# The softmax denominators of a first attention layer: reciprocal on VectorE, or exponential of the negative logarithm on ScalarE

## Chip, cores and metric

The kernel runs on one core of a Trainium2 chip. The metric is the device time of one execution in microseconds (us), shown as the median of several runs.

## What is computed

The reference chains eight blocks, an attention and a feed-forward block in each of four layers, over 8 sequences of 512 tokens with 128 features. Every block is preceded by a layer normalisation and added to its input. Only the first is touched, an attention with 16 heads of 8 features:

```python
scores = einsum('bhqd,bhkd->bhqk', wq, wk) * scale
scores = where(mask, neg, scores)
attn = softmax(scores, axis=-1)
outs.append(einsum('bhqk,bhkd->bhqd', attn, wv))
```

Queries go in windows of 128. The mask is the upper triangle counted from the first key, so query i of any window reaches keys 0 to i of the sequence, never more than its first 128 keys. The other blocks that matter here are a mixture of 8 small experts (two chosen per token), a linear attention with 64 features, whose output is divided by a normaliser, and a mixture of 16 experts (one per token) with a shared expert.

## The kernel before

The first stage (function l0_l1_ffn) takes the eight sequences b through the first four blocks in a software pipeline. Its loop counts steps t; eight steps belong to one sequence, two for each r = 0 to 3; one r covers four heads, one in each quarter of 32 partitions. Generators do the parts, and each step advances the live ones by one yield: `scores` (early), `exps` and `add_up` in the loop itself, `give` (tails), `experts` (gates), `features` (linear), `router` (routers), and `shared` as filler (experts1). The framework turns the program into one queue per engine, with semaphores between them; the order within a queue need not be the written one.

Steps of one sequence, with their lines:

- `scores`: normalise, project, then for each 128 queries PE makes scores (L489), ACT copies them out of PSUM (L495, sm), POOL masks them (L496), DVE takes the maxima (L500). The maxima are transposed (L507, mxT).
- `exps(b, r)`: PE makes the transposed scores less their maximum (L519, sT), ACT takes the exponential (L526, eT, two of 128x1024), POOL masks (L528).
- `add_up(b, r, i)`: PE multiplies eT by the values (i = 0, vq) or by ones (i = 1, own) into two PSUM banks, o0 and o1 (L542). After r = 3, o0 is the weighted sum of the values and o1 holds the softmax sums, repeated over each head's eight rows.
- `give(b)`: DVE inverts o1 into rd (L550) and multiplies by o0 into aT (L552); PE projects (L557), DVE adds to the residual (L558) and takes statistics.
- `experts(b)`: among its steps a Sqrt on ACT (L604), the choice of two experts on DVE (L566 to L577, ending in w, L635), the exponential of w (L637), DVE steps that write the gate tile we (L645), a Silu (L658).
- `features(b)`: the linear attention; its normaliser is clamped (L767) and inverted by DVE (L770), then POOL multiplies (L771).
- `router(b)`: small DVE steps count the rows (L814 to L819), then POOL scatters them with four indirect DMAs (L823).

The scores, the exponentials and the features all go through one PSUM tag of two pairs of banks ("two"). Ten DMAs of zeros (L842) and the loads of later weights (L848) stand on SP's queue in the same stage; the first ten read tile we.

ScalarE holds one table of functions at a time. Where the next function needs another one, the profile has a row ACT_TABLE_LOAD, with the line of the instruction that it serves.

Of the kernel before, what the change touches and what calls it, by code (L numbers as in the profile page):

```python
# [17 lines left out]
AF = mybir.ActivationFunctionType  # L18
# [48 lines left out]
def eight_layers(ctx: ExitStack, tc: tile.TileContext, w: dict, out: bass.AP):  # L67
    nc = tc.nc
# [171 lines left out]
    def cols(c):  # L240
        return slice(c * P, (c + 1) * P)

    def stats(b, mv, x=None):

        x = X[b] if x is None else x
        for c in range(C):
            st = small.tile([P, 6], F32, tag="bn", name="bn", bufs=4)
            nc.vector.bn_stats(st, x[:, c, :])  # L248
            nc.vector.bn_aggr(mv[:, b * C + c, :], st)
# [20 lines left out]
    def l0_l1_ffn():  # L270
# [28 lines left out]
        with ExitStack() as es:  # L299
# [27 lines left out]
            def mm_four():  # L327
                return mm_tile().rearrange("p (c d) -> p c d", c=C)
# [69 lines left out]
            with ExitStack() as es1:  # L398
# [112 lines left out]
                sums_of = {}  # L511
# [35 lines left out]
                def give(b):  # L547
                    ready.pop(b)
                    rd = work.tile([P, S], F32, tag="rd", name="rd", bufs=2)
                    nc.vector.reciprocal(rd, sums_of.pop((b, 1)))  # L550
                    aT = work.tile([P, S], F32, tag="aT", name="aT", bufs=2)
                    nc.vector.tensor_tensor(aT, rd, sums_of.pop((b, 0)), ALU.mult)  # L552
                    yield True
                    yield True
                    pr = mm_four()
                    for k in range(C):
                        nc.tensor.matmul(pr[:, k, :], aT[:, cols(k)], a0["Wo"], start=True, stop=True)  # L557
                    nc.vector.tensor_tensor(X[b], X[b], pr, ALU.add)  # L558
                    stats(b, mv1)
                    gates.append(experts(b))  # L560
                    yield True
# [274 lines left out]
                while t < N * NB or waiting or early or tails or gates or linear or routers:  # L836
# [12 lines left out]
                    b, s = divmod(t, N)  # L849
                    r = s // 2  # L850
                    if s % 2 == 0:
                        if 0 <= b < NB:
                            waiting[b, r] = exps(b, r)
                        step(tails)
                        step(gates)
                        old = (b, r - 1) if r else (b - 1, 3)
                        if old in waiting:
                            add_up(*old, 0, waiting.pop(old))
                            if old[1] == 3:
                                tails.append(give(old[0]))  # L860
                                step(tails)
                        step(routers)
                        step(linear)
                        step(early)
                    else:
                        step(early)
                        step(tails)
                        step(gates)
                        step(routers)
                        step(linear)  # L870
                        if (b, r) in waiting:
                            add_up(b, r, 1, waiting[b, r])
# [1047 lines left out]
```

## Time and profile before

| | |
|---|---|
| median of 3 runs | 1764.63 us (1763.21 to 1764.7) |
| the profiled execution, its own time | 1759.35 us |
| its span, first to last instruction | 1757.6 us |
| busy, share of the span | PE 86%, DVE 67%, ACT 45%, POOL 39% |
| mean granted TensorE clock | 0.94 |

Busy time is an average over stages with different limits; the first stage ends, with the last scatter of `router`, near 660 us, and its attentions near 480 us. A row of the timeline has the start, the length, the engine, the line, the operation with its tiles, and in brackets the engine's idle time just before it with what ended that. Rows of the groups give the total busy time, the mean of one instruction in ns, and the idle time before them.

### The profile page before, as it was taken

The page shows a single profiled execution, that of the slowest core. Times are in us where ns is not written, and L with a number is a line of the kernel's source. Part 1 is how long each engine was busy: PE and PEld are TensorE (multiplying, and loading weights), DVE is VectorE, ACT ScalarE, POOL GpSimd, SP SyncE. Part 2 cuts the span into 40 slices and gives each one's busy share as a digit, 9 for nine tenths or more (in the row PEclk, how much of TensorE's full clock was granted, in tenths as well). Part 3 has the DMA queues.
Part 4 walks back from the last instruction along what each step waited for, and adds up shares of the span by engine and source line. Part 5 has one row for each costly group of instructions (what it writes and reads, how often), then busy time and mean ns, then how long its engine had stood idle before and what let it go on. Part 6 is the DMA issues. An engine that isn't in the chain of part 4 may idle for free.

```text
span 1757.6 us, 23028 instructions
## 1 busy us (share of the span) xinstructions
PE 1505.0 (86%) x8389; PEld 675.3 (38%) x8389; DVE 1169.2 (67%) x2274; ACT 787.2 (45%) x1144; POOL 677.2 (39%) x729
## 2 busy tenths in 40 slices
PE   6978898899898786767999899787988988998877
PEld 2322334344444433544555454332222222333335
DVE  5657546545564443235677675569999999998865
ACT  4545645456454341224233123025655655655644
POOL 5644343344332122021112523425556546632670
PEclk8989998989989998987899899899999999999999
DMA  7991000000000002731554374354444444443301
GB/s 256 384 340 28 1 1 1 13 19 12 6 13 19 18 31 84 219 89 27 131 123 116 98 157 104 91 120 130 132 132 130 129 131 130 129 121 100 81 13 31
DMA packets 98946, 170.96 MB, mean 97 GB/s; under 512 B 11592, under 2 KB 41680, under 8 KB 94736
## 3 DMA queue, kind: packets, MB, share of 16 engines
q1 hardware_dynamic: 94112, 158.20, 32.0%
q0 software_dynamic: 3568, 9.18, 1.7%
q10 hardware_dynamic: 1152, 2.10, 0.4%
q8 instruction: 66, 1.08, 0.2%
q14 instruction: 48, 0.39, 0.1%
HBM read 116.50 MB, written 52.95 MB: 96 GB/s over the span
## 4 chain that ended last, share of the span: by engine, by line
PE 48%; DVE 24%; issue 9%; ACT 6%; SPq 6%; POOL 5%; DMA 2%; DVEq 0%; POOLq 0%; ACTq 0%
DVE h L1827 11%; PE key L1581 5%; PE acc L1559 5%; SPq L842 5%; PE bx L1816 3%; PE sT L519 2%; PE gu L366 2%; PE mm L262 2%; PE Z L1627 2%; PE mm L1187 2%; PE o L542 1%; DVE zx L1635 1%; PE mm L673 1%; PE qq L731 1%; DVE rd L770 1%
## 5 line engine op out<-in xcount | busy, mean ns | idle before, releaser
L1827 DVE TENSOR_TENSOR_SCAN h<-a,bx 128x1024 f32<-128x1024 f32 x192 | 426.3, 2267 | 18.1 <-PE bx L1816 18.1
L1822 ACT ACTIVATE a<-dr,nA 128x1022 f32<-128x1022 f32 x192 | 219.4, 1146 | 213.4 <-DVE h L1827 213.3
L1816 PE MATMUL bx<-gx,wb 64*128 64x512 f32 x768 | 217.9, 658 | 65.9 <-DVE h L1827 63.0
L1272 POOL TENSOR_TENSOR gx<-gx,xk 128x1024 f32<-128x1024 f32 x32 | 75.4, 2357 | 211.7 <-DMA gx<-du_d 208.4
L1581 PE MATMUL key<-xT,L_ffn_keys 128*128 128x512 f32 x256 | 137.4, 619 | 21.9 <-DVE act L1585 21.9
L1816 PEld LDWEIGHTS bx<-gx,wb 64*128 64x128 f32 x768 | 63.6, 191 | 199.4 <-DVE h L1827 157.1
L1559 PE MATMUL acc<-act,L_ffn_values 128*128 128x512 f32 x256 | 133.2, 604 | 0.0
L1585 DVE SCALAR_TENSOR_TENSOR act<-key,gate 128x512 f32<-128x512 f32 x128 | 86.4, 685 | 48.1 <-PE key L1581 38.4
L500 DVE TENSOR_REDUCE mx<-sm 128x8 f32<-128x1024 f32 x64 | 75.9, 1212 | 56.1 <-POOL sm L496 56.1
L1627 PE MATMUL Z<-h,wc 64*32 64x512 f32 x1536 | 110.8, 630 | 1.1 <-DVE h L1827 1.1
L528 POOL TENSOR_SCALAR_AFFINE_SELECT eT<-eT 128x1024 f32<-128x1024 f32 x64 | 68.6, 1095 | 102.3 <-ACT eT L526 102.2
L1370 POOL DMA_INDIRECT back<-f_out,back_at x32 | 30.8, 963 | 168.4 <-DVE bn L248 138.1
L496 POOL TENSOR_SCALAR_AFFINE_SELECT sm<-sm 128x1024 f32<-128x1024 f32 x64 | 69.0, 1095 | 67.4 <-ACT sm L495 67.0
L495 ACT COPY sm<-sc 128x1024 f32<-128x1024 f32 x64 | 62.6, 1014 | 46.5 <-PE sc L489 27.6
L526 ACT ACTIVATE eT<-sT 128x1024 f32<-128x1024 f32 x64 | 62.0, 1019 | 39.8 <-PE sT L519 39.6
L1581 PEld LDWEIGHTS key<-xT,L_ffn_keys 128*128 128x128 f32 x256 | 47.5, 197 | 74.3 <-issue 37.8
L1347 ACT COPY oT<-acc 128x512 f32<-128x512 f32 x8 | 4.7, 586 | 158.0 <-PE acc L1559 158.0
L1559 PEld LDWEIGHTS acc<-act,L_ffn_values 128*128 128x128 f32 x256 | 49.5, 195 | 60.5 <-issue 60.0
L489 PE MATMUL sc<-kb,qT 32*128 32x512 f32 x256 | 55.1, 698 | 18.9 <-ACT eT L526 10.2
L519 PE MATMUL sT<-qT,kb 32*128 32x512 f32 x256 | 55.7, 683 | 9.1 <-ACT sm L495 7.3
L248 DVE BATCH_NORM_STATS2 bn<-x 128x6 f32<-128x128 f32 x224 | 56.2, 272 | 6.3 <-DMA x<-in_L_attn_hidden_states 5.3
L1053 POOL TENSOR_TENSOR rstd<-rstd,minus_half 128x4 f32<-128x4 f32 x27 | 28.0, 1039 | 77.6 <-DVE rstd L1052 77.4
(460 smaller groups left out, 3076.1 us busy)
## 6 DMA issues: line engine op xcount, KB each, us to landing
f_in<-we SPq DMA_DIRECT2D x10, 3584.0 KB
gate<-gates SPq DMA_DIRECT2D x128, 256.0 KB
dr<-dt_d SPq DMA_DIRECT2D x32, 1024.0 KB
gx<-du_d SPq DMA_DIRECT2D x128, 128.0 KB
wt<-in_L_ffn_experts SPq DMA_DIRECT2D x48, 192.0 KB
xk<-xh_d SPq DMA_DIRECT2D x32, 256.0 KB
xg<-f_in SPq DMA_DIRECT2D x48, 64.0 KB
f_out<-ys SPq DMA_DIRECT2D x12, 256.0 KB
```

The source lines that it names most:

```text
L496: nc.gpsimd.affine_select(out=sm, in_=sm, compare_op=ALU.is_ge, fill=-1e30, base=0, pattern=[[0, 8], [-1, P]], channel_multiplier=1,)
L500: nc.vector.tensor_reduce(mx[:, c, 2 * i : 2 * i + 2, 0:4], sm.rearrange("p (q r) k -> p q r k", q=2), AX.X, ALU.max, negate=True,)
L519: nc.tensor.matmul(halves[q // 2][:, q % 2, :], lhs[quad(q), r, :], rhs[quad(q)], start=(k == 0), stop=(k == 1),)
L842: nc.sync.dma_start(rows_in[per * (t - 1) : per * t, :].rearrange("(p n j) d -> p n (j d)", p=P, j=4), we.rearrange("p c k e -> p (c k e)" ...
L1272: nc.gpsimd.tensor_tensor(gx, gx, xk.unsqueeze(1).to_broadcast([P, 2, S]), ALU.mult)
L1559: nc.tensor.matmul(acc, f2_v[:, j, :], act, start=(j == 0), stop=(j == J - 1))
L1581: nc.tensor.matmul(key, f2_k[:, 2 * j : 2 * j + 2, :], xT, start=True, stop=True)
L1585: nc.vector.scalar_tensor_tensor(act, key, 0.0, gate[:, j % 2, :], ALU.max, ALU.mult)
L1627: nc.tensor.matmul(zs[q][32 * j : 32 * j + 32, i, :], wcf[half, g, :], hs[j // 2][half, j % 2, :], start=(g == 0), stop=(g == G - 1),)
L1816: nc.tensor.matmul(bx[:, k, :], wbf[half, g, :], gx[half, j, :], start=True, stop=True,)
L1822: nc.scalar.activation(a[:, :, 1:], dr[:, 2 * j : 2 * j + 2, 1:], AF.Exp, scale=nA[:, q, g : g + 1],)
L1827: nc.vector.tensor_tensor_scan(h.rearrange("p r t -> p (r t)"), a.rearrange("p r t -> p (r t)"), bx.rearrange("p r t -> p (r t)"), 0.0, AL ...
```

## The change

In `give`, DVE's reciprocal of the softmax sums becomes two ACT instructions: the natural logarithm from PSUM into rd, then in place the exponential of its negative, since exp(-ln s) = 1/s. The multiply that follows stays on DVE. The diff has this one place; the second attention's reciprocal (L770) is as before.

```diff
                 def give(b):
                     ready.pop(b)
                     rd = work.tile([P, S], F32, tag="rd", name="rd", bufs=2)
-                    nc.vector.reciprocal(rd, sums_of.pop((b, 1)))
+
+                    nc.scalar.activation(rd, sums_of.pop((b, 1)), AF.Ln)
+                    nc.scalar.activation(rd, rd, AF.Exp, scale=-1.0)
                     aT = work.tile([P, S], F32, tag="aT", name="aT", bufs=2)
                     nc.vector.tensor_tensor(aT, rd, sums_of.pop((b, 0)), ALU.mult)
```

## The prediction

> **What bounds the kernel now.** I read the table of stages first, then the rows of the one line that the change takes away, then the timeline around each of its eight executions, and last the chain of work that ended last. The change touches only the first stage, the one in which the attentions of the first layer run through their eight sequences, from 0 to about 480 us. These are the stage's rows after the first transfers; the columns are length, then busy time of PE, PEld, DVE, ACT and POOL with instruction counts, granted clock, DMA share and GB/s:
>
> ```profile
> 60.00:132.00 72.00, 60.20 (x347) 21.79 (x346) 46.40 (x97) 35.26 (x42) 37.90 (x41) 0.88 1.02 356
> 132.00:165.00 33.00, 26.52 (x136) 9.32 (x137) 22.45 (x41) 18.07 (x24) 13.80 (x14) 0.90 0.14 35
> 165.00:220.00 55.00, 48.53 (x298) 20.92 (x297) 33.09 (x80) 31.80 (x40) 24.19 (x26) 0.94 0.00 1
> 220.00:294.00 74.00, 67.04 (x427) 28.41 (x424) 38.09 (x96) 37.67 (x46) 26.82 (x29) 0.91 0.00 1
> 294.00:369.00 75.00, 67.38 (x439) 29.93 (x440) 41.17 (x115) 38.55 (x50) 31.66 (x34) 0.93 0.04 11
> 369.00:440.00 71.00, 66.63 (x468) 29.26 (x469) 36.85 (x113) 39.98 (x51) 29.32 (x32) 0.98 0.05 16
> ```
>
> Two regimes are seen. Until about 121 us the DMA engines are full (share 1.02). After that PE is busy some 90% of the time, and DVE and ACT a little over half each. So neither the engine that gets lighter nor the one that gets heavier is the bound on average. What counts is where PE stands still because an ACT or DVE result is late, and those places lie at the turn from one sequence to the next, where the reciprocal is. The turn of the sixth sequence, from the timeline of all engines (start, length, engine, line, idle time before it and who ended it):
>
> ```profile
> 340.59 3.35 DVE L550 RECIPROCAL rd<-o 128x512 f32<-128x512 f32 x1
> ...
> 348.87 0.16 DVE L635 TENSOR_TENSOR w<-oh_m 128x4 f32<-128x4 f32 x1
> ...
> 350.23 0.69 PE L710 MATMUL kq<-bf,row 32*128 32x256 f32 x2 [2.35 <-ACT eT L526]
> ```
>
> and from the timeline of ACT alone:
>
> ```profile
> 344.88 1.28 ACT L637 ACT_TABLE_LOAD   x1
> 349.06 0.20 ACT L637 ACTIVATE w<-w 128x4 f32<-128x4 f32 x1 [2.90 <-DVE w L635]
> 349.17 1.92 ACT L526 ACTIVATE eT<-sT 128x1024 f32<-128x1024 f32 x2
> ```
>
> DVE does the 3.35 us reciprocal, then the small steps that choose the experts, and their last, w (L635), comes at 348.87. ACT holds the small exponential of w (L637) ahead of the two large exponentials (L526), so it stands idle for 2.90 us, and PE for 2.35 us behind it. The reciprocal is thus on the path at some turns, though DVE is half idle.
>
> **What goes.** Eight reciprocals, all alike:
>
> ```profile
> L550 DVE RECIPROCAL rd<-o x8: 3345/3348/3358, 64.5 to 467.3; 128x512 f32<-128x512 f32 x8
> ```
>
> DVE loses 8 x 3.35 = 26.8 us. The second attention's reciprocal (L770, also 3.35 us) stays: the diff has one place only.
>
> **What comes.** Eight Ln and eight Exp of 128x512 on ACT. No Ln is in the trace. The nearest rows, with the table loads, are these:
>
> ```profile
> L637 ACT ACT_TABLE_LOAD x7 | 9.0, 1283 | 0.1
> ...
> L1202 ACT ACTIVATE z<-z 128x512 f32<-128x512 f32 x8 | 5.1, 632 | 0.0
> ...
> L265 ACT COPY mxT<-mm 128x512 f32<-128x512 f32 x8 | 4.7, 587 | 8.0 <-PE mm L262 8.0
> ```
>
> Ln reads PSUM and writes SBUF like the copy: 0.59 us. Exp works in place in SBUF like L1202: 0.63 us. Both could lie between the copy's 0.59 and the 0.69 of an activation from PSUM with a bias column (L1201, 688 ns); eight pairs differ by 1.3 us at most by that, which I neglect. The larger part is the table loads, 1.28 us each. Before every change among Sqrt, Exp and Silu the trace has a load, 76 in all. I assume Ln has a table of its own, so one load before Ln and one before the Exp. Seven of the eight places are lucky for the second: L604 (Sqrt) loads before the reciprocal and the next exponential reloads behind it (second to seventh sequence: 91.39 and 98.22, 139.93 and 146.76, 189.08 and 200.38, 255.20 and 269.89, 329.58 and 344.88, 402.46 and 413.86), so for six of them the reload only moves forward. The first place stands among exponentials (+2), and in the eighth the next load is for Silu (475.00), so its reload is extra too (+2). Ten loads more, 86. ACT gets 6 x 2.50 + 2 x 3.78 = 22.6 us.
>
> What a switch costs besides the load: at 139.93 the load starts 0.02 us after the activation before it ends, and the Sqrt starts 0.01 us after the load, so nothing. The Trainium skill (ScalarE: Activation LUTs, What ACT_TABLE_LOAD costs) adds a drain of about 1.38 us to every switch, 2.66 us in all; this trace doesn't show it. By that figure the cost summed below would be some 3.5 us higher (half of 1.38 at five turns) and the time about 1763; as the rows around 139.93 leave no room for it, it gets no chance of its own.
>
> **Sequence by sequence.** The first two turns (64.5 and 93.9 us) lie ahead of this row:
>
> ```profile
> 120.82 0.26 DVE L645 TENSOR_TENSOR we<-oh 128x96 f32<-128x96 f32 x1 [12.62 <-DMA L_ffn_shared_gate_w<-in_L_ffn_shared_gate_w]
> ```
>
> DVE stands 12.6 us until the transfers that read tile we are through. Those run back to back on SP's queue (L842, some 9.4 us each) and wait for no engine's work here. What ACT loses (3.78 and 2.50) or DVE gains (2 x 3.35) before that is swallowed; I cost it at 0. If that cover were gone, it would be between -6.7 and +6.3.
>
> *Gain at the others.* The most that can be had is the idle time of ACT in front of w, and no more than 3.35: third sequence 3.35 (idle 6.37 at 154.41), fourth 1.48 (at 203.15), fifth 2.99 (at 274.16), sixth 2.90, seventh 0 (there the exponentials went at 415.15 ahead of w). In the eighth the reciprocal is itself a link of the chain that ended last:
>
> ```profile
> 467.36 3.26 DVE rd L550
> 470.65 0.59 DVE x L777
> ```
>
> Behind it DVE makes the row numbers (L814 to L819) for POOL's four scatters (L823, 475.31 to 484), and L639, DVE's L645 and PE at 485.94 (idle 6.69) wait behind those: 3.35. Together 14.1. In the fifth and sixth, two reduces (L500) that wait for POOL's masks also stand ahead of w, so what is late next is POOL; I take half there, 1.50 and 1.45. That leaves 3.35 + 1.48 + 1.50 + 1.45 + 3.35 = 11.1 us.
>
> *Cost at the others.* Ln waits for the sums of PE (L542, own), then stands in ACT's queue with the masked scores' copies (L495), the copies L694 and the large exponentials behind it; POOL's masks, DVE's maxima and, through the two PSUM pairs that scores and exponentials share, PE wait for those. ACT's idle gaps around the place are 1.76 + 0.54 in the third sequence before its long wait, 5.1 in the fourth, 3.0, 4.1 and 2.7 in the next three, so 2.50 would nearly fit each time; but single gaps are 0.3 to 1.8 us and a load is 1.28. Bounds: 0 when all fits, 2.50 x 5 = 12.5 when nothing does. I take half, 6.3, being as near to one as to the other. In the eighth a gap of 3.02 us before 471.13 takes most of it: 0 (bound 3.78). The multiply L552 waits for Exp now; Ln, load and Exp in a row take 2.5 us against 3.35, so it is not later as long as ACT starts at once.
>
> **Sum.** -11.1 + 6.3 = -4.8 us. Against the profiled execution (1759.35, of which 1757.6 is the span) 1754.5; the median shown is 5.3 higher, so 1764.6 - 4.8 = **1759.8**. All routers end before the expert stage can start, so a shift of this stage should reach the end whole.
>
> **Rivals.**
> *ACT becomes the late one (slower).* The pieces don't fit the gaps, and POOL's masks, not the reciprocal, hold w. Each turn then pays up to 2.50 and the last 3.78: 16.3 at most, 1780.9, and some 1773 if half is paid and nothing gained. It decides from the point where the copies L495 after a turn start over 1.3 us later while L637 still idles as long. For it: DVE waits for POOL sm and POOL for ACT sm through most of the stage (36.1 and 35.3 us between 160 and 440). Against: ACT's gaps add up to more than 2.50 at four turns of five.
> *It cancels.* Gain and cost within 3 us: 1764.6. For it: PE is 90% busy, so at most some 8 us a sequence can be won at all.
> *One load serves both.* If the load before Ln brings a table that holds Exp too, no load is added in the six middle turns and two in the other places: 78 loads, 1.22 us of ACT a turn, half paid at five turns 3.1, and 11.1 - 3.1 = 8.0 faster, 1756.6. The loads of before can't tell, as they have no Ln. The Trainium skill (ScalarE: Activation LUTs, Table sets: the hidden batching unit) names a set with both and counts one load for ln followed by exp; no run here shows which set is taken.
> *The order changes.* PE's instructions do not run in the written order (at 337.6 to 340.2 the products L542 of the old sequence run ahead of L519 of the new one, written first), so the program's order follows expected durations, and new ones can shuffle a turn. One misplaced w costs 6.4 us, as in the second and third sequence; either sign.
>
> **How the numbers follow.** Forecast 0.40 (0.36 faster, 0.04 same), ACT late 0.32 (slower), cancels 0.16 (same), one load 0.07 (faster), order 0.05 (0.02 faster, 0.03 slower). Faster 0.45, same 0.20, slower 0.35, where same is within 0.2%, 3.5 us, about what can be told from no change here. The forecast's own range is 1750.5 (all 14.1, no cost) to 1763. The slower case reaches 1781; cutting its far end, 1750 to 1777 leaves under 2 in 10 out.
>
> **What would show it.** Right: 86 table loads, Ln near 590 ns, Exp near 632, DVE 26.8 us less and ACT 22.6 more; ACT's idle time in front of w shorter in the third to sixth sequence; the scatters of the eighth turn some 3 us earlier against its L542; the gate at 120.8 unmoved. Wrong: 78 loads; PE's waits for ACT sm (L495) grown by more than its waits for eT (L526) shrink; w still held by the reduces L500; the shift won by 480 us lost again before 660.

## The result, and the profile after

The changed kernel takes 1742.10 us (median of 4 runs, 1737.14 to 1747.94), beside 1763.92 before (4 runs): a ratio of 0.9881, 95% interval 0.9848 to 0.9914, 21.8 us faster. In a second comparison it was 0.9892 (0.986 to 0.9923). The forecast was 1759.8, 1750 to 1777: the sign is as forecast, the size more than four times as large, and the time lies below the range. Line numbers of the changed kernel are those of before plus 2 from the multiply on: L551 is Ln, L552 the exponential, L554 the multiply, L560 the addition to X (L558 before), L639 the exponential of w (L637 before).

The two new lines, from the trace of after by line and shape (duration in ns: least, median, most; first and last start):

```profile
L551 ACT ACT_TABLE_LOAD  x8: 1283/1283/1283, 70.9 to 452.1; - x8
L551 ACT ACTIVATE rd<-o x8: 597/597/598, 72.2 to 453.4; 128x512 f32<-128x512 f32 x8
...
L552 ACT ACT_TABLE_LOAD  x8: 1283/1283/1283, 72.8 to 454.5; - x8
L552 ACT ACTIVATE rd<-rd x8: 629/630/630, 74.1 to 455.8; 128x512 f32<-128x512 f32 x8
```

Sixteen instructions with sixteen loads, in all 86 loads against 76. ACT's busy time rises from 787.2 to 809.3 us, DVE's falls from 1169.2 to 1143.1. All this is as forecast.

The time is won between the third and the eighth addition to X. One row each of the table of stages, over just that stretch (columns as in the prediction: length, busy time of PE, PEld, DVE, ACT, POOL, granted clock, DMA share, GB/s). Before:

```profile
165.96:485.20 319.24, 285.46 (x1924) 125.89 (x1924) 172.06 (x481) 166.88 (x212) 127.89 (x139) 0.94 0.02 8
```

After:

```profile
165.89:464.34 298.45, 275.86 (x1923) 119.53 (x1924) 160.06 (x477) 176.94 (x226) 127.00 (x138) 0.98 0.02 8
```

Both stretches start at the same time, 165.9, and after's is 20.8 us shorter. The number to see is PE's: the same 1924 matmuls are busy for 9.6 us less, although the change gives PE nothing and takes nothing from it. The third number from the end goes with it: the granted clock is 0.94 before and 0.98 after. Below I call (1 - granted clock) x length the *time lost to the clock*; summed over the single turns (a turn is the stretch from one addition to X to the next) it is 19.2 us before and 6.7 after. By this measure 12.5 of the 20.8 us are clock, and 8.3 are other waits. The measure also counts low clock in which PE stands idle; PE's busy time alone shows 9.6, so the clock's part is some 10 to 12 us here.

The sixth turn, which the prediction showed for before, in after, from the timeline:

```profile
326.77 1.28 ACT L551 ACT_TABLE_LOAD   x1
328.07 0.60 ACT L551 ACTIVATE rd<-o 128x512 f32<-128x512 f32 x1
...
328.84 1.28 ACT L552 ACT_TABLE_LOAD   x1
330.13 0.63 ACT L552 ACTIVATE rd<-rd 128x512 f32<-128x512 f32 x1
...
332.79 0.15 DVE L637 TENSOR_TENSOR w<-oh_m 128x4 f32<-128x4 f32 x1
332.98 0.20 ACT L639 ACTIVATE w<-w 128x4 f32<-128x4 f32 x1 [1.31 <-DVE w L637]
...
334.13 0.70 PE L519 MATMUL sT<-qT,kb 32*128 32x512 f32 x2 [1.29 <-ACT sm L495]
```

The four pieces take 4.0 us from the first start to the last end, but ACT's wait for w is 1.31 us instead of 2.90, and PE's wait (now for a copy L495, before for the exponentials L526) is 1.29 instead of 2.35. What follows the wait is the larger difference. Before, in three pieces: up to PE's wait, the wait, and the stretch behind it:

```profile
346.00:347.90 1.90, 1.89 (x14) 1.36 (x12) 1.90 (x6) 0.16 (x1) 0.00 (x0) 1.00 0.00 0
347.90:350.20 2.30, 0.00 (x0) 0.00 (x0) 1.77 (x16) 1.14 (x3) 0.52 (x1) 1.00 0.00 0
350.20:359.00 8.80, 8.07 (x44) 5.50 (x46) 3.33 (x17) 3.51 (x5) 6.97 (x9) 0.61 0.07 24
```

After, the same three:

```profile
329.00:331.70 2.70, 2.69 (x12) 0.68 (x4) 2.02 (x14) 2.65 (x3) 0.12 (x1) 1.00 0.01 3
331.70:334.10 2.40, 1.13 (x4) 0.30 (x4) 2.40 (x12) 1.12 (x3) 1.17 (x2) 1.00 0.00 0
334.10:343.00 8.90, 8.82 (x70) 5.44 (x70) 5.01 (x16) 5.69 (x8) 5.55 (x7) 1.00 0.07 24
```

Before, PE does nothing for 2.30 us, and in the next 8.8 us its clock is granted at 0.61: 44 matmuls. The 0.61 is a mean; cut finer, the clock is near 1.00 (0.98) until 351.2, and then

```profile
351.20:358.00 6.80, 6.38 (x39) 4.90 (x40) 2.64 (x14) 1.51 (x3) 5.20 (x7) 0.50 0.09 31
```

So the clock is halved for 6.8 us. After, the wait is half as long, the clock stays at 1.00, and 70 matmuls (not all of the same kind) go through in the same time. By this estimate one stall of 2.30 us cost 2.30 + 8.80 x 0.39 = 5.7 us. The Trainium skill (TensorE: Matmul & The Clock Gate, HAM oscillation) puts the bound for a harmless gap of PE at some 3.4 us; here a gap of 2.30 us was followed by the low clock, and the row decides. The Trainium skill (same page, A second HAM failure mode: psum-queue depth-cycling) also says that frequent short idles between groups of matmuls make the clock go up and down; the low clock behind a gap of 2.30 us points the same way.

The eighth turn, from PE's timeline before:

```profile
485.94 1.22 PE L663 MATMUL mm<-wT,sel 32*128 32x512 f32 x1 [6.69 <-DVE x L558]
```

and after:

```profile
464.23 1.54 PE L665 MATMUL mm<-wT,sel 32*128 32x512 f32 x3
```

PE's largest wait of the stretch (6.69 us) is gone. In before the addition stood in DVE's queue behind the gate tile, the gate tile waited for POOL's step w (L639), and that stood in POOL's queue behind all four scatters. From POOL's timeline before:

```profile
483.03 0.96 POOL L823 DMA_INDIRECT f_in<-xr,to  x1 [1.53 <-DMA f_in<-xr,to]
484.06 0.23 POOL L639 TENSOR_SCALAR w<-w 128x4 f32<-128x4 f32 x1
```

and after, where the same step (now L641) comes behind the first of the four:

```profile
456.46 1.12 POOL L825 DMA_INDIRECT f_in<-xr,to  x1 [2.18 <-DVE to L821]
457.62 0.26 POOL L641 TENSOR_SCALAR w<-w 128x4 f32<-128x4 f32 x1
```

So in after the addition starts at 464.34, before the last of the four scatters (464.47). This is a change in the order of POOL's queue, to which e7 below comes back. The granted clock from 479 to 494 was 0.56 before; from 465 to 475 it is 1.00 after.

From there the gain runs through: the last scatter moves from 675.11 to 653.74, by 21.4 us. This profiled execution of after (1746.86) is a long one: against that of before it lost 9 us again in the later layers, which the change doesn't touch and where two executions of before differ by 19 (its four runs are 1737.1, 1737.3, 1746.9 and 1747.9, with mean clocks of 0.943, 0.941, 0.937 and 0.936).

### The profile page after: what moved, and what is told of

Same layout as the page of the kernel before. It is cut to its first block, busy times and chain, and to the rows that moved or that the text cites. A ratio compares the mean times of both kernels' runs of the same rounds, so it can differ in the third digit from the quotient of the medians.

```text
span 1745.2 us, 23011 instructions
## 1 busy us (share of the span) xinstructions
PE 1509.6 (86%) x8389; PEld 674.4 (39%) x8389; DVE 1143.1 (66%) x2266; ACT 809.3 (46%) x1170; POOL 677.6 (39%) x729
## 4 chain that ended last, share of the span: by engine, by line
PE 49%; DVE 23%; issue 9%; ACT 7%; POOL 7%; DMA 4%; SPq 1%; DVEq 0%; POOLq 0%; ACTq 0%
DVE h L1829 11%; PE key L1583 5%; PE acc L1561 5%; PE sT L519 4%; PE bx L1818 3%; PE mm L262 2%; PE o L542 2%; PE gu L366 2%; PE sc L489 2%; DMA gx<-du_d 1%; PE Z L1629 1%; PE mm L1189 1%; DVE xn L347 1%; DVE zx L1637 1%; PE qq L733 1%
## 5 line engine op out<-in xcount | busy, mean ns | idle before, releaser
L1583 PE MATMUL key<-xT,L_ffn_keys 128*128 128x512 f32 x256 | 138.0, 622 | 21.8 <-DVE act L1587 21.7
L1372 POOL DMA_INDIRECT back<-f_out,back_at x32 | 30.9, 965 | 168.5 <-DVE bn L248 138.2
L495 ACT COPY sm<-sc 128x1024 f32<-128x1024 f32 x64 | 62.9, 1011 | 46.8 <-PE sc L489 33.7
L526 ACT ACTIVATE eT<-sT 128x1024 f32<-128x1024 f32 x64 | 62.3, 1021 | 46.5 <-PE sT L519 46.2
L519 PE MATMUL sT<-qT,kb 32*128 32x512 f32 x256 | 59.5, 702 | 12.8 <-ACT sm L495 11.2
```

The lines of the kernel that those rows point to most:

```text
L519: nc.tensor.matmul(halves[q // 2][:, q % 2, :], lhs[quad(q), r, :], rhs[quad(q)], start=(k == 0), stop=(k == 1),)
L1583: nc.tensor.matmul(key, f2_k[:, 2 * j : 2 * j + 2, :], xT, start=True, stop=True)
```

## The experiments

The theories. **A**: DVE's shorter queue ends the waits of the turns sooner, and ACT's two instructions cost something. **C**: on top of A, PE loses clock behind its waits, and shorter waits win that back. **S**: the program's order of instructions has changed, and the new one happens to be better. In the programs as they are built, by the shortest difference of the two orders, 5 of PE's 4512 instructions stand elsewhere in after than in before, 65 of DVE's some 2270, and 16 of POOL's 738. So PE's own order hardly changed, but DVE's and POOL's did.

The table has the stretch from the third to the eighth addition to X in the profiled execution of each kernel, the clock loss in it, and the ratio of times to before.

| kernel | third addition, us | 3rd to 8th, us | lost to the clock | rest | ratio (95%) |
|---|---|---|---|---|---|
| before | 166.0 | 319.2 | 19.2 | 300.0 | 1 |
| before again | 164.7 | 318.4 | 17.6 | 300.8 | 0.9966 (0.9938-0.9994) |
| after | 165.9 | 298.5 | 6.7 | 291.8 | 0.9881 (0.9848-0.9914) |
| after again | 167.8 | 301.8 | 10.9 | 290.9 | 0.9892 (0.986-0.9923) |
| e1 no inversion | 171.8 | 302.9 | 12.3 | 290.6 | 0.9901 (0.9872-0.9929) |
| e2 copies | 171.1 | 292.2 | 0.0 | 292.2 | 0.9895 (0.9842-0.9948) |
| e3 both | 166.3 | 320.5 | 17.5 | 303.0 | 1.0019 (0.9988-1.005) |
| e4 dense PE | 166.5 | 314.8 | 7.2 | 307.6 | 0.999 (0.9963-1.0017) |
| e5 exp of w late | 151.0 | 301.7 | 4.7 | 297.0 | 0.9845 (0.9791-0.9899) |
| e6 second too | 167.8 | 316.8 | 17.7 | 299.1 | 1.0075 (1.005-1.01) |
| e7 DVE load back | 169.7 | 313.0 | 17.3 | 295.7 | 0.9968 (0.9945-0.999) |
| e8 after, exp of w late | 153.0 | 297.2 | 6.6 | 290.6 | 0.9795 (0.9738-0.9851) |
| e9 second only | 165.2 | 308.4 | 15.6 | 292.8 | 0.9971 (0.9948-0.9994) |

The row "before again" is the same kernel as before: 0.3% is what the comparison leaves between two equal kernels, so ratios within that of 1 say nothing. The clock loss comes from one profile for each row; it differs by 1.6 us between the two profiles of before and by 4.2 between the two of after.

**e1, no inversion.**

```diff
-                    nc.vector.reciprocal(rd, sums_of.pop((b, 1)))
+                    nc.vector.tensor_scalar(rd, sums_of.pop((b, 1)), 0.0, 0.015625, ALU.mult, ALU.add)
```

> The inversion is left out: in place of the reciprocal DVE writes a constant into rd (one tensor_scalar from PSUM, about 0.68 us), ACT gets nothing. DVE is relieved by 2.7 us a turn, there is no Ln, no Exp and no extra table load. Theory A (only the stalls of the forecast: gain 11.1, ACT's cost 6.3): the cost is gone, so about 6 us faster than the changed kernel, some 1736. Theory C (the gain is mostly TensorE's granted clock, which drops to half after a stall at a turn; what ACT gets is nearly free): the same as the changed kernel, 1737 to 1748, and the time lost to the clock, that is the sum of (1 - granted clock) x length, over turns 4 to 8 (from the L558 add of the third sequence to that of the eighth) falls from 19 us to under 8. Theory S (a lucky order of instructions that came with the new instructions): this kernel's order is close to that of before, so 1755 to 1765.

1745.64 us, the time that C gave, and neither A's 1736 nor S's 1755 to 1765. ACT has nothing new, and yet nearly the whole gain is there, so Ln and the exponential are not needed for it. The clock loss is 12.3 us, though, where C had said under 8. And the order is not that of before on every engine: PE differs from before in 5 instructions, but POOL in 14, and from after POOL differs in 5 only; in the eighth turn its step w (472.77) is ahead of the last two scatters here too. So this run shows that relief of DVE comes with the gain, not that it does so at before's order.

**e2, copies in place of Ln and exponential.**

```diff
-                    nc.scalar.activation(rd, sums_of.pop((b, 1)), AF.Ln)
-                    nc.scalar.activation(rd, rd, AF.Exp, scale=-1.0)
+                    nc.scalar.activation(rd, sums_of.pop((b, 1)), AF.Relu, scale=0.015625)
+                    nc.scalar.activation(rd, rd, AF.Relu, scale=0.5)
```

> The changed kernel with two Relu (scaled) in place of Ln and Exp, so the inversion is left out: the same two ACT instructions of 128x512, but no table loads for them (10 loads, 12.8 us of ACT fewer). Theory A: 3 to 6 us faster than the changed kernel, as its cost term came from the loads that do not fit ACT's gaps. Theory C: within 4 us of the changed kernel, as the loads lie in gaps. Theory S: anything between 1735 and 1765, not tied to the clock.

1744.55 us, against 1745.89 of after in the same comparison, with an order close to after's (3 of PE's instructions stand elsewhere, 25 of DVE's, 3 of POOL's). Without its clock loss the stretch takes 292.2 us, after's 291.8 and 290.9. The loads of the new pairs (77 in all here, 86 in after) cost nothing that can be measured, and A's 3 to 6 us did not come.

**e3, ACT's pair added, DVE's reciprocal kept.**

```diff
+                    both = sums_of.pop((b, 1))
+                    nc.vector.reciprocal(rd, both)
+                    nc.scalar.activation(aT, both, AF.Ln)
+                    nc.scalar.activation(aT, aT, AF.Exp, scale=-1.0)
```

> The kernel before with its reciprocal kept on DVE, and Ln and Exp done as well, into tile aT ahead of the multiply that overwrites it: ACT's cost without DVE's relief. Theory A: 3 to 10 us slower than before (1767 to 1774). Theory C: within 4 us of before, and the half-clock stretches of turns 4 to 8 as before (16 to 22 us lost). Theory S: faster than before by 10 us or more would show that new ACT instructions alone make the better order.

1767.98 us, 3.8 above before, with 1 inside the interval: ACT's pair alone, in an order of its own, costs between -2 and 9 us by that interval and gains nothing, and the clock is lost as in before. The 3.8 us lie in the range of A and in that of C, so this run doesn't tell the two apart.

**before again and after again.**

> The kernel before once more, for a second profile of it. If the half-clock stretches of the turns belong to this kernel (theory C: they follow the stall of PE at each turn, where it stands for DVE's reciprocal), the clock lost in the turns four to eight is again 15 to 22 us, against 7 to 12 in the two profiles of after, and their length is within 5 us of 319. If they come and go with the execution (the rival: chance), the loss may be anywhere between 0 and 20, and the comparison of single profiles says little.

17.6 us lost: the loss in these turns belongs to the kernel. Each turn agrees with the first profile within 1.7 us. Of after a second profile was made too. By theory C it was to lose under 8 us, and 15 or more would have ended C; it lost 10.9. So the two kernels differ in this loss by 6.7 to 12.5 us, by which pair of profiles is taken.

**e4, dense matmuls in PE's wait.**

```diff
+                    if r == 0:
+                        sums_of[b, 1] = ps.tile([P, S], F32, tag="o1", name="o1", bufs=1)
+                        for _ in range(3):
+                            nc.tensor.matmul(
+                                sums_of[b, 1], to_all[:, 0, :], mxT, start=True, stop=True
+                            )
```

> The kernel before, with three more matmuls of 128x128 by 128x512 per sequence behind the softmax's row of maxima in the first attention, into a tile that the sums overwrite later: 24 matmuls of some 0.25 to 0.5 us, so 6 to 12 us of added PE work, none of it wanted, in the stretch where PE otherwise waits. Nothing is taken from DVE. Theory C (part of the gain is the clock that PE loses behind its waits at a turn): the clock lost in the turns four to eight falls from 19 us to under 8, and the time is between 10 us faster and 5 slower than before, although work was added. Rival (the gain is DVE's shorter queue alone, the clock follows something else): the loss stays at 15 to 20 and the time is 5 to 13 us slower.

Each added matmul shows as two records, 48 in all, 24 of them in the stretch; six together, from PE's timeline:

```profile
339.15 2.84 PE L526 MATMUL o<-mxT,to_all 128*128 128x512 f32 x6
```

and the row of the stretch:

```profile
166.52:481.33 314.81, 283.79 (x1948) 123.00 (x1948) 174.61 (x481) 166.91 (x212) 127.66 (x139) 0.98 0.02 8
```

At 0.47 us a record, 48 are 23 us of added PE work, twice what I had expected, and 11 us lie in the stretch. The loss falls from 19.2 to 7.2 us, while the rest grows from 300.0 to 307.6, and the time is that of before. So work that nobody wants was added to PE at no cost in time, while the clock held. That is what C asks for. It does not show how much of after's gain is clock; and the order changed here too, if little (8 of DVE's instructions and 2 of POOL's stand elsewhere), which the run can't take out.

**e5, the exponential of w issued late.**

```diff
-                        nc.scalar.activation(e, halves[i], AF.Exp)
+                        state["eT"] = nc.scalar.activation(e, halves[i], AF.Exp)
...
-                    nc.scalar.activation(w2, w2, AF.Exp)
+                    with tc.issue_after(state["eT"].ins):
+                        nc.scalar.activation(w2, w2, AF.Exp)
```

> The kernel before with the small exponential of L637 issued behind the last large exponential that stands ahead of it, DVE's reciprocal kept: it changes only the order in ACT's queue at the turn. If ACT's order at the turn were what the change gained by (theory S, a luckier order), this would be some 10 us or more faster than before. By theory A (DVE's queue sets the turn) it is within 6 us of before, either way.

1736.11 us: the expectation from A fell. It was said without the gate in mind. From DVE's timeline of e5:

```profile
111.74 0.68 DVE L558 TENSOR_TENSOR x<-x,mm 128x512 f32<-128x512 f32 x1
...
132.17 0.26 DVE L646 TENSOR_TENSOR we<-oh 128x96 f32<-128x96 f32 x1 [0.21 <-DMA L_attn_dw_kernel<-in_L_attn_dw_kernel]
```

In before DVE stood 12.62 us at the gate tile until 120.82, with the second addition to X (123.25) queued behind it. Here the addition is ahead of the gate tile, which comes when the transfers have long read the old one and waits 0.21 us. The third addition is 15.0 us earlier, and the turns behind it lose 4.7 us to the clock instead of 19.2. A better order at another place is thus worth at least as much as the change. It doesn't speak for S in the change itself, where the third addition starts at 165.9 as before.

**e6, the second attention's reciprocal on ACT too.**

```diff
-                    nc.vector.reciprocal(rd, rd)
+                    nc.scalar.activation(rd, rd, AF.Ln)
+                    nc.scalar.activation(rd, rd, AF.Exp, scale=-1.0)
```

> After, with the reciprocal of the second attention (L770 of before) given to ACT as well: eight more pairs of 128x512, so 26.8 us less on DVE and 9.8 us of arithmetic and some 16 table loads more on ACT. If the relief of DVE pays wherever its queue is full (theory A carried on), it is 5 to 15 us faster than after. If the second attention's reciprocals stand where ACT is the later engine (the rival), it is 0 to 10 us slower than after.

1776.21 us, 30 above after and outside both expectations.

**e7, DVE's load given back at after's order.**

```diff
-                    nc.scalar.activation(rd, rd, AF.Exp, scale=-1.0)
+                    nc.scalar.activation(rd, sums_of.pop((b, 0)), AF.Exp, scale=-0.001)
...
-                    nc.vector.tensor_tensor(aT, rd, sums_of.pop((b, 0)), ALU.mult)
+                    nc.vector.reciprocal(aT, rd)
```

> After, with its order of instructions on every engine all but kept, and DVE given back what the change took: the multiplication of 0.68 us becomes a reciprocal of 3.35, while Ln and the exponential stay on ACT (it leaves the denominators out: the exponential reads the numerator, scaled down to near one, and the result has no use for the sums). So ACT's cost and the order are those of after, and DVE has 21 us more, 2.67 at each turn. Theory A (the gain is DVE's shorter queue at the turn, with the clock that follows it): 1758 to 1775 us, and the clock lost in the turns four to eight is back at 13 to 20 us. Theory S (after's order is what gains): 1740 to 1752.

1759.31 us, and 17.3 us lost to the clock. The row for the stretch, beside that of after above:

```profile
169.74:482.74 313.00, 285.37 (x1924) 123.93 (x1924) 170.58 (x477) 177.56 (x226) 128.00 (x139) 0.95 0.02 8
```

PE's order is that of after to the line (19 of DVE's instructions and 7 of POOL's stand elsewhere), and ACT's busy time is the same (177.6 and 176.9). DVE alone has 10.5 us more, and the stretch is 14.6 us longer, 10.6 of them clock, PE's busy time back at 285. The waits that the prediction had in view are back as well: in the fourth to sixth turn ACT stands 3.79, 3.48 and 3.60 us in front of w, where it stood 1.31, under 0.2 and 1.31 in after.

S falls as the whole reason, but it keeps a part. The stretch is still 6.2 us shorter than in before, and 5.4 of that lie in the eighth turn: 54.94 us before, 49.55 here, 48.56 in after. POOL's step w stands behind the first scatter (473.87) as in after, from POOL's timeline of e7:

```profile
475.02 0.25 POOL L641 TENSOR_SCALAR w<-w 128x4 f32<-128x4 f32 x1
```

In all the runs the eighth turn takes 48 to 52 us where this step stands ahead of the last scatters, and 54.9 to 56.3 where it stands behind all four (before twice, e3, e4, e5). So of after's 20.8 us some 15 go with DVE's relief, by A and C, and some 5 with POOL's order at the eighth turn. The split is rough, as the reciprocal of e7 stands behind the exponential and not in its old place.

**e8, after with the edit of e5.**

> After with the edit of e5. In e5 the third addition to X ended 15 us earlier than in before (151.0 against 166.0), as the work behind the router's weights, which land at 120.8, no longer holds the queues between 105 and 121; the change doesn't touch that stretch (165.9 in after). If the two gains lie in different places, they add but for the clock, which both had already won back (14 us in e5, 12 in after, of 19): some 15 us under after, 1726 to 1738, and under e5 by 0 to 10. Rival (both only find the same slack): 1736 to 1746, no better than e5 alone.

1726.75 us (1718.57 to 1738.61), a ratio of 0.9795: faster than before and than after. The gains of the gate and of the change lie in different places: the third addition is early as in e5 (153.0), the stretch short as in after (297.2). They add in part: alone they are 28 and 22 us, together 38. Whether e8 is faster than e5 alone is not certain, as the intervals of the two ratios overlap (4 executions each). In DVE's timeline of e8 the second addition (114.23) is ahead of the gate tile (133.06, a wait of 0.21 us) as in e5.

**e9, the second attention's reciprocal alone on ACT.** The edit of e6, made to before.

> The kernel before with only the second attention's reciprocal (L770) given to ACT; the first attention keeps its own on DVE. Both together (e6) were 30 us slower than after, and POOL's multiplication waited 70 us for ACT there against 31 for DVE. If the second pair is late on ACT by itself (theory: the place decides, and in the second attention ACT is the later engine), it is 2 to 15 us slower than before. If the 30 us came of the two pairs meeting on ACT, or of the order of e6 alone, it is between 12 us faster and 2 slower than before.

1762.94 us, a ratio of 0.9971 (0.9948 to 0.9994): no different from the 0.9966 of before against itself, and the range of my theory missed. But in the trace a gain and a loss cancel. The eighth addition comes at 473.6, 11.6 us earlier than in before (the eighth turn takes 49.0 us, with POOL's step w at 464.19, ahead of the scatters). The last scatter comes at 670.90, only 4.2 us earlier. From the eighth addition to the last scatter e9 takes 197.3 us and e6 198.4; every kernel with the second reciprocal on DVE takes 188.2 to 191.9, before 189.9 and after 189.4. PE's two longest waits there for POOL's multiplication, which stands behind the pair, before:

```profile
560.19 1.16 PE L776 MATMUL mm<-L_attn_Wo,aT 128*128 128x128 f32 x8 [0.76 <-POOL aT L771]
605.80 1.16 PE L776 MATMUL mm<-L_attn_Wo,aT 128*128 128x128 f32 x8 [1.52 <-POOL aT L771]
```

and the same two sequences in e9:

```profile
548.03 1.97 PE L777 MATMUL mm<-L_attn_Wo,aT 128*128 128x128 f32 x8 [2.62 <-POOL aT L772]
598.91 1.69 PE L777 MATMUL mm<-L_attn_Wo,aT 128*128 128x128 f32 x8 [2.89 <-POOL aT L772]
```

So the pair in the second attention does cost time by itself, some 7 to 9 us behind the eighth addition, and the total hid it. With a third wait (1.76 before, 0.58 in e9) these waits grow by 2.1 us in all and PE's busy time by 3.4; the rest of the 7.4 was not traced. POOL's idle time before the multiplication says little: it is 70.4 us, all put down to ACT, but in before it is 68.5 too, of which 30.9 are put down to DVE's rd.

The 30 us of e6 over after are then 18 us in the stretch, 11 of them clock, 9 behind the eighth addition, and 2 ahead of the third. Whether the 18 come of the two pairs meeting on ACT or of e6's order stays open.

## Why the prediction came out as it did

**What goes and what comes: right.** DVE lost 26.1 us (26.8 forecast), ACT gained 22.1 (22.6), 86 loads, Ln 597 ns and the exponential 630. The rival of one load for both falls: each of the eight pairs took two. The Trainium skill (ScalarE: Activation LUTs, Table sets: the hidden batching unit) counts one load for ln followed by exp; this trace has two for each of the eight pairs.

**The first two turns: 1.7 us slower, where I had 0.** The gate came at 118.70 instead of 120.82, but the second addition at 124.97 instead of 123.25. Why is not shown; the bounds that I gave (-6.7 to +6.3) hold it.

**The third turn: 1.8 instead of 3.35.** From the second addition to the third it takes 42.7 us before and 40.9 after, so at the third addition nothing is left of either. The mechanism came as forecast, w's exponential at 150.88 instead of 154.41, but part of what it won was lost to ACT. From the timelines of after:

```profile
143.69 1.28 ACT L551 ACT_TABLE_LOAD   x1
...
147.37 0.63 ACT L552 ACTIVATE rd<-rd 128x512 f32<-128x512 f32 x1
147.90 0.99 ACT L495 COPY sm<-sc 128x1024 f32<-128x1024 f32 x1
...
148.95 2.07 PE L519 MATMUL sT<-qT,kb 32*128 32x512 f32 x4 [2.49 <-ACT sm L495]
```

and from the stages of after:

```profile
148.90:158.00 9.10, 8.03 (x26) 2.61 (x26) 5.53 (x17) 3.74 (x5) 4.55 (x5) 0.50 0.00 0
```

The copy of the masked scores stands behind the pair, PE waits 2.49 us for it, and the clock is 0.50 for the next 9.1 us (in before it was 0.64 from 154 to 163, behind a wait of 4.17). This is the rival "ACT becomes the late one", at one turn of the eight.

**The gains of the fourth to eighth turn: the sizes right, the mechanism only in the fifth and sixth.** Forecast 1.48, 1.50, 1.45, 0 and 3.35, 7.8 in all. Without the clock's part the turns of after are shorter by 1.4, 1.8, 0.8, 0.2 and 4.2 us, 8.3 in all (fourth: 55.70 - 3.3 = 52.4 before, 52.64 - 1.6 = 51.0 after, and so on; the clock has two digits, so each is good to some 0.6). Each term was to come from ACT's idle time in front of w. In the fifth and sixth turn that did shrink, from 2.99 to under 0.2 and from 2.90 to 1.31, and in e7 it is back. In the fourth it went from 1.48 to 1.31 only, and in e7, where ACT stands 3.79 us there, the turn without its clock is as short as in after (51.0); that this term fits is luck. In the eighth I had the four scatters 3.35 us earlier and the addition still behind them. What happened is that POOL's step w went ahead of three of them; with DVE's load given back (e7) all but 1.0 us of the gain stays. That term fits by luck too.

**The cost on ACT: mis-sized.** I took 6.3 us, half of what it would be if nothing fitted. Besides the third turn nothing of it shows: e2, which has no loads for its pair, is no shorter than after without the clock, and e1, which has no pair at all (but keeps 0.68 us a turn on DVE), is shorter by 0.3 to 1.2 us. The gaps were there; I had added them up (5.1, 3.0, 4.1, 2.7) and still halved the bound by the size of single gaps.

**The clock: absent from the sum.** This is the step that failed. "One misplaced w costs 6.4 us" counted the wait alone, and a gain of ACT's idle time was taken as the whole gain. But before had 19.2 us of lost clock in the five turns. Of these, 10.2 lie behind three waits of PE at the turns (1.43 us for a copy L495 at 199.50, 2.43 and 2.35 for the exponentials at 275.33 and 350.23), 2.2 in the eighth turn, and 6.8 behind three waits of 1.20 us for ACT's qf (L736) some 25 us further on. After has 6.7: 5.1 behind waits for qf, 1.7 behind one for DVE at 178.09, and nothing behind the turn's waits for sm and eT. The prediction's own table of stages showed 0.91 and 0.93 in the rows 220 to 294 and 294 to 369, and I read them as properties of the stage. With the measured sizes in their place the sum is: gains 7.8, cost 0, clock 12.5, together 20.3, and the time 1744. That is hindsight: the trace of before has the 19.2, but not how much of it would go.

**The order.** I gave it 0.05. On DVE and POOL the order changed, and e5 shows that an order can be worth 28 us. Here it made some 5 us, at the eighth turn, as e7 shows; that it did not make the rest is seen from e7 alone, as e1 has nearly after's order on POOL. A run of the relief at before's order on POOL too was not made, so the split stands on one run.

**Stays open.** Why the clock falls behind one wait and not behind another of nearly the same length is not settled: in before a wait of 2.93 us that ended at 178.51 was followed by a clock of 1.00 for 22 us, one of 2.35 that ended at 350.23 by 0.50 from 351.2 on; and the wait of 1.20 us for ACT's qf at 226.8 in before was followed by the low clock (0.50 from 228.3 to 235.1), while the same wait at 223.7 in after was not (1.00). In the e4 run most of the clock held with work in the wait; it doesn't show what bound the wait has to stay under.

## What to carry to other kernels

Price a wait of PE with what its clock does behind it: cut the stretch after each wait into windows, and count (1 - granted clock) x length as part of the wait's cost; here it was as much as the waits themselves. An engine that is half idle can still be worth relieving where its queue stands before such a wait, and moving 2.5 us of work to another half-idle engine was free where that engine's gaps added up to it; in the second attention the same move cost 7 to 9 us. Since any edit may reorder the whole program, keep one experiment that makes the edit's effect at the old order, and one that undoes it at the new, and compare the order of every engine's queue, not of PE's alone. And where a total does not move, look whether a gain and a loss cancel in it, as in e9.

## What the hardware showed that was not expected

PE's clock went to half (0.50, for 6.8 us from 351.2 in before) behind a single wait of 2.35 us and stayed at 1.00 behind one of 2.93, and PE's busy time for the same 1924 matmuls changed with it from 285.5 to 275.9 us. Of the four executions of after, the two shorter ones have the higher mean clock: 1737.1 us at 0.943, 1747.9 at 0.936. A switch of tables on ACT cost its load of 1.28 us and no more: at 146.07 the load for L552 begins 0.01 us after the copy before it ends, and the exponential begins 0.02 us after the load.
